# Moving VectorE's two-SBUF-operand additions, and one batch's weight sums, to GpSimd in the softmax stage of a transformer block

## The chip, the cores and the metric

The kernel runs on one core of one Trainium2 chip. A core has a matrix engine (TensorE, "PE" in the profile; its weight loads are listed as "PEld"), three engines for elementwise work (VectorE "DVE", ScalarE "ACT", GpSimd "POOL") and SyncE ("SP"), which here only issues transfers. Each engine runs its own instructions in the order in which the program lists them, and waits on semaphores for the others. The metric is the device time of one execution in microseconds. Three runs of the kernel before took 3894.92, 3904.91 and 3907.19 us.

## The reference

Input x has 8 sequences of 512 tokens by 1024 features, all float32. Four residual steps follow one another, each on a layer norm of what came before:

```python
x = x + attn_a(layernorm(x), qkvw, qkvb, ow, ob)   # 32 heads of 32, softmax over 512 keys
x = x + ffn(layernorm(x), weight, bias, centroids, assignments)
x = x + attn_b(layernorm(x), bv_q, bv_k, bv_v)     # 4 heads of 256, causal, sigmoid in place of softmax
x = x + ffn(layernorm(x), weight, bias, centroids, assignments)

def ffn(h):
    dots = softmax(h @ centroids.T / 0.1)           # 64 clusters
    hits = dots > 0.01
    return where(any(hits, 1)[:, None] & any(hits over all tokens)[assignments], h @ weight.T + bias, 0)
```

The change concerns the first line, the softmax attention: the products for q, k and v (1024 by 3072 weights), scores, softmax, values, the output product with `ow` (1024 by 1024) and its bias, and the first layer norms on both sides of it.

## The kernel before, in words

**Products.** The large products use a scheme of seven products in place of eight for a 2 by 2 split of both factors (`LEFT`, `RIGHT`). Its sums of blocks are `left_sums` and `right_sums`, four additions each; `gather` and `done` add each finished product from PSUM (`acc`) into the outputs that need it. For q, k and v the scheme is nested twice, the inner one over the outer one's nodes. The sums on the side of the weights are made once, while batch 0 runs, and stored to memory: `weight_sums` (L649) for six column groups ("jobs") and two halves `c` each, with lines L669 and L681 as its additions and L672 to L687 its stores.

**The softmax stage** is one generator, `softmax_attention`. It runs 64 units `n`: 8 batches of 8 groups of 4 heads (`NC` = 8 units a batch, g = n % 8), some 41.5 us each. The loop over units (from L1262) does four steps i in each:

- `rows_step(n+1, i)`: TensorE makes 128 rows of scores of the next unit (L1097) in the PSUM tile `sc`, and VectorE takes each row's maximum, `nmax` (L1098);
- `between()`: a share of the auxiliary work, see below;
- at i = 0, `turn_max(n)`: TensorE turns the maxima (`tpm`), of which `split_max` (L1104 to L1108, GpSimd) has made bf16 parts at the end of the unit before; ScalarE casts the result to `shift`;
- `keys_step(n, i)`: TensorE writes the shift (L1126) and the transposed scores (L1129) into `sc`, and ScalarE takes the exponential, `pT` (L1131). `sc` has one PSUM buffer (of four banks), so rows and keys take turns in it;
- `sum_step(n, i)`: GpSimd adds the four `pT` of a unit into `sum` (L1141), two 128x1024 halves at a time. The last sum, and `split_max(n+1)` ahead of it, stand at the end of the unit;
- at i = 0 and 2, `values_step` (L1152) and, at i = 0, `normalize(n-1)`: denominators, reciprocal, and the context `ctx_s` with its bias.

**Auxiliary work** fills the time that a softmax unit leaves on TensorE. `filler` is a queue of pieces with weights (about 0.86 for a matmul group, 0 for work without one); each `take()` runs a fixed share of the queue's total weight (`FILLER_SHARES`). It holds the q, k and v products of coming units and the output products of the batch before. `mix` puts the pieces of a finished row tile's layer norm at given positions of the queue, counted in entries. Two other queues, `side` and `slow`, hold the next batch's layer norm in turned form (`norm_tasks`: load four row tiles, statistics, root, shift, store and spread the per-token factors, load the turned tile, then eight GpSimd operations L628 that scale it). `sums` holds the weight sums, of which each `between` runs one entry.

**The output products.** `out_pair(q)` handles two row tiles, so 14 pairs within the stage and two more at its end. It loads x into `r`, adds the bias `ob_s` (L959), makes the four c sums of the context (L975, two or three `c` tiles and one in place in `ctx_s`), runs seven products and adds them in `done`: `t` (named `ct` in the profile) is a partial result that goes into three quarters of the outputs, r += t (L978). `leave(m)` then stores a finished tile as x1 (L1006) and hands it to the norm (`norm_pieces`, with ScalarE's `rescale` at L264 and the shift at L271). With `OUT_SHARES` = (3, 2, 0, 2) products a unit, leave(0) falls at the end of units with n % 4 = 2 and leave(1) at the end of those with n % 4 = 0, n = 10 to 56, twelve each; the norm of a tile runs in the odd unit behind it.

**The order of GpSimd's instructions** is thus the order in which the generator emits them. At the end of a unit it is: x1 store if there is one, split_max, the two halves of the last sum; the next unit's norm and left sums (L1214) follow.

Both weight streams (`w`, 6 buffers, and `ow`, 5 buffers) are loaded by SyncE's queue, one block for each block that is done.

Of the kernel before, what the change touches and what calls it, by code (L numbers as in the profile page):

```python
# [55 lines left out]
class Consts:  # L56
# [3 lines left out]
    def __init__(self, nc, pool):  # L60
# [3 lines left out]
        nc.vector.memset(self.nhalf, -0.5)  # L64
        self.ones = pool.tile([P, P], F32, name="ones")
# [131 lines left out]
def right_sums(nc, b11, b12, b21, b22, t1, t2, t3, t4):  # L197

    tt = nc.vector.tensor_tensor
    return [  # L200
        partial(tt, t1, b12, b11, ALU.subtract), partial(tt, t2, b22, t1, ALU.subtract),
        partial(tt, t4, b21, t2, ALU.subtract), partial(tt, t3, b22, b12, ALU.subtract),
    ]
# [38 lines left out]
class Stage:  # L242


    def __init__(self, tc, cst, small, ps_m):
        self.tc, self.nc, self.cst, self.small, self.ps_m = tc, tc.nc, cst, small, ps_m

# [6 lines left out]
    def rstd(self, mv, n, r=None):  # L254
# [3 lines left out]
        self.nc.vector.tensor_scalar(r, mv[:, :, 1], EPS, None, ALU.add)  # L258
# [10 lines left out]
    def shifts(self, mv, r, out):  # L269

        self.nc.vector.scalar_tensor_tensor(out, mv[:, :, 0], -1.0, r, ALU.mult, ALU.mult)  # L271
# [57 lines left out]
class Clusters:  # L329
# [41 lines left out]
    def softmax(self, b):  # L371

        nc, small, st = self.stage.nc, self.stage.small, {}
# [5 lines left out]
        def first():  # L379
            top = small.tile([P, TPB], F32, tag="top", name="top")  # L380
            nc.vector.tensor_reduce(top, lg, AX.X, ALU.max)
            nc.vector.tensor_tensor(lg, lg, wide(top), ALU.subtract)
# [4 lines left out]
        def second():  # L387
# [3 lines left out]
            nc.vector.tensor_tensor(lg, lg, wide(den), ALU.mult)  # L391
# [5 lines left out]
        def fourth():  # L397
# [3 lines left out]
            else:  # L401
                some = self.pool.tile([P, NCL], F32, tag="some", name="some")
                nc.vector.tensor_reduce(some, turned, AX.X, ALU.max)
                nc.vector.tensor_max(self.hits, self.hits, some)
# [26 lines left out]
def softmax_attention(tc, cst, stage, filler, clusters, pools, dr, late, args):  # L431
# [28 lines left out]
    units, half = B * NC, NC // 2  # L460
    ctx_s = ctxp.tile([P, SLOTS, half, 2 * P], F32, name="ctx_s")
# [87 lines left out]
    side, slow, tiles, waiting, ready, held = deque(), deque(), deque(), deque(), deque(), []  # L549
# [40 lines left out]
    def norm_tasks(b):  # L590
# [35 lines left out]
        def apply(k, j):  # L626
# [5 lines left out]
            [partial(load, i) for i in range(TPB)],  # L632
            [idle, *(partial(stats, i) for i in range(TPB))],
            [root, partial(turned, 0), shift, partial(turned, 1), send],
            [partial(turned, 2), partial(turned, 3), spread, idle],
# [13 lines left out]
    def weight_sums(kind, job, c):  # L649
# [4 lines left out]
        def load():  # L654
            xs = [npool.tile([P, H], F32, tag=tag, name=f"wx_{kind}_{job}_{c}") for tag in ("n1", "nT")]
# [8 lines left out]
        def outer(k):  # L664
            b21, t4, t2, b12 = (st["x"][i][:, a] for i in range(2) for a in range(2))
            b11, b22 = st["y"][:, 0], st["y"][:, 1]
            if k == 0:
                st["steps"] = right_sums(nc, b11, b12, b21, b22, b11, t2, b12, t4)
            st["steps"][k]()  # L669
            if k == 0:  # L670
                once = dr.once[kind, job].rearrange("p (k c n) -> c p k n", k=2, c=2)
                nc.gpsimd.dma_start(once[c], b11)  # L672

        def again(i, k):
            x = st["x"][i].rearrange("p a k (j n) -> p a k j n", j=2)
            b11, b12, b21, b22 = (x[:, :, kk, j, :] for kk in range(2) for j in range(2))
            if k == 0:
                z = rpool.tile([P, H], F32, tag="r", name=f"wz_{kind}_{job}_{c}_{i}")
                z = st["z"] = z[:, : 3 * 2 * P].rearrange("p (m a n) -> p m a n", m=3, a=2)
                st["more"] = right_sums(nc, b11, b12, b21, b22, z[:, 0], z[:, 1], b12, z[:, 2])  # L680
            st["more"][k]()  # L681
            dst = dr.twice[kind, job, i].rearrange("p (m a c n) -> c a p m n", m=7, a=2, c=2)[c]
            if k == 2:
                for a in range(2):
                    nc.gpsimd.dma_start(dst[a, :, 4:], st["z"][:, :, a, :])
            if k == 3:
                for a in range(2):  # L687
                    nc.gpsimd.dma_start(dst[a, :, :4], x[:, a].rearrange("p k j n -> p (k j) n"))
                if c == 1 and i == 1:
                    stored.add((kind, job))  # L690

        def outers():
            for k in range(4):
                outer(k)

        def agains():
            for i in range(2):
                for k in range(4):
                    again(i, k)

        return [load, lambda: None, outers, agains]
# [89 lines left out]
    def job_pieces(kind, n, part):  # L791
# [24 lines left out]

        def twice(i, k, at):
            def go():
# [13 lines left out]
                weights.done(at)  # L832

# [12 lines left out]
        def done(node, j, acc):  # L846
# [5 lines left out]
            if node == 0:  # L852
                (ia, ja), (ib, jb) = of(0), of(1)
# [3 lines left out]
                add(jb, ib)  # L857
                add(ja, jb, qb)
# [69 lines left out]
    def ow_sum_tasks(c):  # L928
# [8 lines left out]
        def step(k):  # L937
            if k == 0:
                t = [csp.tile([P, half, P], F32, tag=f"c{m}", name="cbox").rearrange("p c t -> p (c t)") for m in range(4)]
                st["t"] = (t[0], t[1], t[3], t[2])  # L940
                st["steps"] = right_sums(nc, st["B11"], st["B12"], st["B21"], st["B22"], *t)
# [5 lines left out]
    def out_pair(q, pools, base, last):  # L947
# [10 lines left out]
        def bias(m):  # L958
            nc.vector.tensor_tensor(r[m], r[m], ob_s, ALU.add)  # L959
# [7 lines left out]
        def sums():  # L967
            a11, a12, a21, a22 = quarters()
            names = (sums_pool.tile([P, half, P], F32, tag=f"c{k}", name=f"c{k}_{q}") for k in range(3))
            st["left"], st["steps"] = left_sums(nc.vector, a11, a12, a21, a22, *names)  # L970
# [6 lines left out]
        def add(out, what):  # L977
            nc.vector.tensor_tensor(out, what, out, ALU.add)  # L978

        def done(k):  # L980
# [7 lines left out]
            elif k == 1:  # L988
                add(st["t"], acc)
                add(r[0][:, b], st["t"])  # L990
# [3 lines left out]
            elif k == 6:  # L994
                add(r[0][:, b], acc)
                leave(0)
            elif k == 3:
                add(st["t"], acc)
                add(r[1][:, a], st["t"])
                add(r[1][:, b], st["t"])  # L1000
            else:
                add(r[1][:, a], acc)
                leave(1)

        def leave(m):
            nc.gpsimd.dma_start(dr.x1[first + m], r[m])  # L1006
# [22 lines left out]
        before = {0: [zero(a11)], 2: [zero(load, 1)], 3: [zero(bias, 1)]}  # L1029
        products = [before.get(idx, []) + [(0.86, mm(idx, c)) for c in range(half)] for idx in range(7)]  # L1030
        for k in range(4):
            products[1].insert(2 * k + 1, zero(some_sum, k))
# [902 lines left out]
```

## Time and profile before

The profiled execution took 3899.21 us, of which 3897.5 us are the span shown in the profile. It is 0.15% below the median of the three runs.

| | us | share of the span |
|---|---|---|
| TensorE busy | 3675.3 | 94% |
| VectorE busy | 2569.3 | 66% |
| GpSimd busy | 1634.9 | 42% |
| ScalarE busy | 940.5 | 24% |
| granted TensorE clock, mean | 0.984 | |

Softmax stage: about 0 to 2720 us. The remaining 1178 us are the later steps of the block.

| stretch, us | TensorE busy | granted clock |
|---|---|---|
| 0 to 320 | 286.99 | 0.98 |
| 320 to 500 | 152.47 | 0.92 |
| 500 to 2460 | 1840.78 | 0.99 |
| 2460 to 2720 | 232.76 | 0.97 |
| 2720 to 3897 | 1162.29 | 1.00 |

In lines of the profile, `sc<-qk,qk` is an output and its inputs by the program's names, the numbers that follow are partitions by elements. In a line of the waits, the three numbers are the total in us, how many, and the longest. In a line of a group, `| 31.8, 2119 |` is busy time in us and the mean of one in ns, then the idle time ahead of them and what ended it. In a line of the timeline, the first two numbers are the start and the length in us, and the brackets hold the idle time just before and what released it.

### The profile page before, as it was taken

The page shows a single profiled execution, that of the slowest core. Times are in us where ns is not written, and L with a number is a line of the kernel's source. Part 1 is how long each engine was busy: PE and PEld are TensorE (multiplying, and loading weights), DVE is VectorE, ACT ScalarE, POOL GpSimd, SP SyncE. Part 2 cuts the span into 40 slices and gives each one's busy share as a digit, 9 for nine tenths or more (in the row PEclk, how much of TensorE's full clock was granted, in tenths as well). Part 3 has the DMA queues.
Part 4 walks back from the last instruction along what each step waited for, and adds up shares of the span by engine and source line. Part 5 has one row for each costly group of instructions (what it writes and reads, how often), then busy time and mean ns, then how long its engine had stood idle before and what let it go on. Part 6 is the DMA issues. An engine that isn't in the chain of part 4 may idle for free.

```text
span 3897.5 us, 81316 instructions
## 1 busy us (share of the span) xinstructions
PE 3675.3 (94%) x34228; PEld 1929.0 (49%) x34228; DVE 2569.3 (66%) x3649; ACT 940.5 (24%) x1047; POOL 1634.9 (42%) x1378
## 2 busy tenths in 40 slices
PE   8998899999999999999999999998999999999999
PEld 4345454545545454454544445533444457774444
DVE  4657666677667757667675766665698864556666
ACT  1222222222222222222222222323111134431000
POOL 2875565466455545635554563443000034540000
PEclk9999999999999999999999999999999999999999
DMA  5657756666665665766566565536566667774332
GB/s 178 179 173 236 230 163 188 190 180 176 180 188 145 206 182 168 207 160 177 160 204 178 156 182 158 145 114 195 188 175 178 175 185 226 224 232 146 130 129 97
DMA packets 756954, 690.11 MB, mean 177 GB/s; under 512 B 327912, under 2 KB 563440, under 8 KB 756592
## 3 DMA queue, kind: packets, MB, share of 16 engines
q1 hardware_dynamic: 725328, 575.07, 52.4%
q0 software_dynamic: 26944, 94.13, 6.6%
q10 hardware_dynamic: 4320, 15.73, 1.0%
q8 instruction: 271, 4.44, 0.5%
q14 instruction: 91, 0.75, 0.1%
HBM read 537.94 MB, written 146.83 MB: 176 GB/s over the span
## 4 chain that ended last, share of the span: by engine, by line
PE 79%; DVE 12%; DMA 4%; issue 2%; POOL 2%; ACT 1%; SPq 0%; DVEq 0%; ACTq 0%; POOLq 0%
PE mm L647 31%; PE dense L1496 20%; PE av L1152 6%; PE sc L1129 5%; PE sc L1097 5%; DVE nmax L1098 4%; PE o L1577 3%; PE csc L1558 3%; PE sc L1126 2%; DMA w<-in_qkvw 2%; DVE r L978 1%; PE logitsT L349 1%; PE den L1191 1%; DVE qk L842 1%; DVE r L959 1%
## 5 line engine op out<-in xcount | busy, mean ns | idle before, releaser
L1131 ACT ACTIVATE pT<-sc 128x2048 f32<-128x2048 f32 x256 | 480.6, 1878 | 1246.8 <-PE sc L1129 1235.6
L1141 POOL TENSOR_TENSOR sum<-sum,pT 128x1024 f32<-128x1024 f32 x256 | 613.2, 2417 | 332.9 <-ACT pT L1131 332.8
L1098 DVE TENSOR_REDUCE nmax<-sc 128x4 f32<-128x2048 f32 x256 | 585.1, 2285 | 156.3 <-PE sc L1097 156.2
L1141 POOL TENSOR_TENSOR sum<-pT,pT 128x1024 f32<-128x1024 f32 x128 | 325.7, 2568 | 546.6 <-ACT pT L1131 305.8
L647 PE MATMUL mm<-xT,w 128*64 128x128 f32 (+6 forms) x4164 | 390.8, 344 | 22.6 <-DMA w<-in_qkvw 20.1
L647 PEld LDWEIGHTS mm<-xT,w 128*64 128x64 f32 (+2 forms) x4164 | 229.2, 132 | 188.2 <-issue 112.2
L647 PE MATMUL mm<-s,w 128*64 128x256 f32 (+3 forms) x3288 | 288.1, 351 | 25.8 <-issue 13.1
L1097 PE MATMUL sc<-qk,qk 32*64 32x512 f32 x4096 | 289.3, 621 | 1.7 <-ACT pT L1131 1.5
L1129 PE MATMUL sc<-qk,qk 32*128 32x512 f32 x2048 | 270.5, 601 | 0.0
L163 DVE TENSOR_TENSOR u<-dense,u 128x512 f32<-128x512 f32 x223 | 148.0, 685 | 185.0 <-PE dense L1496 169.5
L647 PE MATMUL mm<-ow,ctx_s 128*64 128x512 f32 (+2 forms) x1168 | 262.3, 600 | 4.4 <-DMA ow<-o_T 3.9
L647 PEld LDWEIGHTS mm<-s,w 128*64 128x64 f32 (+1 forms) x3288 | 175.5, 129 | 179.9 <-issue 68.0
L1152 PE MATMUL av<-pT,v 128*32 128x512 f32 x2048 | 255.8, 619 | 0.0
L1496 PE MATMUL dense<-sum,s 128*128 128x512 f32 x512 | 231.8, 593 | 0.0
L647 PEld LDWEIGHTS mm<-e,w 128*64 128x64 f32 (+1 forms) x3456 | 178.6, 134 | 84.8 <-issue 41.6
L647 PE MATMUL mm<-e,w 128*64 128x128 f32 (+1 forms) x3456 | 206.5, 278 | 11.8 <-DVE qk L163 6.5
L163 DVE TENSOR_TENSOR qk<-mm,qk 128x256 f32<-128x256 f32 x392 | 157.9, 417 | 80.2 <-PE mm L647 72.9
L647 PE MATMUL mm<-w,xT 128*64 128x128 f32 (+4 forms) x2816 | 194.0, 296 | 3.7 <-DMA w<-t_v 3.7
L1126 PE MATMUL sc<-shift,ones_h 32*128 32x512 bf16 x1024 | 102.8, 390 | 98.7 <-DVE nmax L1098 91.8
L163 DVE TENSOR_TENSOR v<-mm,v 128x256 f32<-128x256 f32 x196 | 78.6, 417 | 164.5 <-PE mm L647 159.3
L647 PEld LDWEIGHTS mm<-w,xT 128*64 128x64 f32 (+2 forms) x2816 | 150.8, 133 | 63.3 <-issue 29.3
L647 PE MATMUL mm<-ow,c 128*64 128x512 f32 (+2 forms) x816 | 178.2, 597 | 2.1 <-DMA ow<-o_T 2.1
(267 smaller groups left out, 5501.6 us busy)
## 6 DMA issues: line engine op xcount, KB each, us to landing
w<-t_qk SPq DMA_DIRECT2D x392, 256.0 KB, 3.5
ow<-o_T SPq DMA_DIRECT2D x240, 256.0 KB, 4.0
w<-in_qkvw SPq DMA_DIRECT2D x216, 256.0 KB, 4.5
w<-t_v SPq DMA_DIRECT2D x196, 256.0 KB, 2.8
ow<-in_ow SPq DMA_DIRECT2D x180, 256.0 KB, 3.2
dT_a<-xT SPq DMA_DIRECT2D x32, 512.0 KB, 6.2
x_a<-x SPq DMA_DIRECT2D x32, 512.0 KB, 7.9
x<-x_a POOLq DMA_DIRECT2D x32, 512.0 KB, 4.5
```

What stands on the lines that cost most here:

```text
L163: nc.vector.tensor_tensor(out, acc, other, ALU.add)
L647: nc.tensor.matmul(out[cols], lhsT[:, cols], rhs, **flags)
L1097: nc.tensor.matmul(sc[ts(j, P // 2), h, :], st["q"][rows, cols], st["k"][rows, :], start=True, stop=True)
L1098: nc.vector.tensor_reduce(st["nmax"][:, qt, :], sc, AX.X, ALU.max, negate=True)
L1126: nc.tensor.matmul(sc[:, h, :], cst.ones_h[rows, :], st["shift"][rows, :], start=True, stop=False)
L1129: nc.tensor.matmul(sc[:, h, :], st["k"][rows, ts(kt, P)], st["q"][rows, :], start=False, stop=True)
L1131: nc.scalar.activation(pT, sc, AF.Exp, scale=SCALE_A)
L1141: nc.gpsimd.tensor_tensor(st["sum"][:, h, :], before[:, h, :], st["pT", kt][:, h, :], ALU.add)
L1152: nc.tensor.matmul(st["av"][rows, :], st["v"][:, kt, rows], pT[:, h, :], start=(kt == 0), stop=(kt == TPB - 1))
L1496: nc.tensor.matmul(st["acc"], st["left"][LEFT[k]][:, c, :], self.w[RIGHT[k]][:, c, :], start=(c == 0), stop=(c == half - 1),)
L1558: nc.tensor.matmul(sc[:, AT_OFF[i] : AT_OFF[i] + n], k[:, c, ts(i, P)], xT[:, c, i * P :], start=(c == 0), stop=(c == 1),)
L1577: nc.tensor.matmul(acc[:, j - jj, :], at[:, start : start + P], self.v[b * TPB + i][:, cols], start=(i == 0), stop=(i == j),)
```

## The change

Within the softmax stage, these parts move or are rewritten:

- `stage.few` is GpSimd while the stage runs and VectorE after it: the addition of eps, the layer norm's shift (now two multiplications, with constants `eps` and `minus`), and the subtraction, scaling and collecting of the cluster softmax.
- `weight_sums`: its additions go to GpSimd, its nine stores a half from GpSimd's queue to SyncE's; they are paced in three entries a (job, c) instead of four, and c = 1 uses other buffers.
- Batch 0 (n < 8): the additions of kt = 2 and 3 in `sum_step` become one 128x2048 addition on VectorE; that of kt = 3 stands in the next unit, ahead of its first rows_step.
- Nested node 0: VectorE adds from PSUM alone; four additions of 128x256 a pair or group (`join`) are left for GpSimd, emitted at the next `between` or before the outer node 0 is added.
- `out_pair`, for the 14 pairs of the stage: the four c sums go to GpSimd and from product 1, where they were spaced out, to the start of product 0. The additions of `t` into the three quarters (`join`) and the bias go to GpSimd and stand in `done` and `leave`, just before the store of x1.
- The sums of `ow` go to GpSimd.
- The loads, statistics and turned loads of the next batch's norm are spread differently over four entries.
- The turned tile of a finished row tile is fetched at filler position 26 instead of 20.

In instructions: VectorE goes from 3168 to 2735, GpSimd from 1013 to 1488, SyncE from 1883 to 1990; TensorE and ScalarE keep theirs, with a few in another order.

```diff
 # class Stage, rstd and shifts
-        self.nc.vector.tensor_scalar(r, mv[:, :, 1], EPS, None, ALU.add)
+        self.few.tensor_tensor(r, mv[:, :, 1], self.cst.eps[:, :n], ALU.add)
         self.nc.gpsimd.tensor_tensor(r, r, self.cst.nhalf[:, :n], ALU.pow)
...
-        self.nc.vector.scalar_tensor_tensor(out, mv[:, :, 0], -1.0, r, ALU.mult, ALU.mult)
+            self.few.tensor_tensor(out, mv[:, :, 0], self.cst.minus[:, : mv.shape[1]], ALU.mult)
+            self.few.tensor_tensor(out, out, r, ALU.mult)
 # softmax of clusters
-            nc.vector.tensor_tensor(lg, lg, wide(top), ALU.subtract)
+            few.tensor_tensor(lg, lg, wide(top), ALU.subtract)
 # norm_tasks
-            [partial(load, i) for i in range(TPB)],
-            [idle, *(partial(stats, i) for i in range(TPB))],
-            [root, partial(turned, 0), shift, partial(turned, 1), send],
-            [partial(turned, 2), partial(turned, 3), spread, idle],
+            [partial(load, 0), idle, partial(load, 1), idle, partial(load, 2)],
+            [partial(stats, 0), partial(load, 3), partial(stats, 1), partial(stats, 2), idle],
+            [partial(stats, 3), partial(turned, 0), root, partial(turned, 1), shift],
+            [send, partial(turned, 2), spread, partial(turned, 3), idle],
 # weight_sums
-                st["steps"] = right_sums(nc, b11, b12, b21, b22, b11, t2, b12, t4)
+            for step in right_sums(nc.gpsimd, b11, b12, b21, b22, b11, t2, b12, t4):
+                step()
...
-                nc.gpsimd.dma_start(once[c], b11)
+            nc.sync.dma_start(dr.once[kind, job].rearrange("p (k c n) -> c p k n", k=2, c=2)[c], st["y"][:, 0])
 # job_pieces
+        def join(j, side):
+            nc.gpsimd.tensor_tensor(target(side, j)[:, 1], target(1, j)[:, side == 0], target(side, j)[:, 1], ALU.add)
...
+                if all(len(m) == 7 for m in made):
+                    soon.extend(partial(join, j, side) for j in range(2) for side in (1, 0))
...
-                add(jb, ib)
-                add(ja, jb, qb)
+                add(jb, acc)
+                add(ja, acc, qb)
 # out_pair
         def bias(m):
-            nc.vector.tensor_tensor(r[m], r[m], ob_s, ALU.add)
+            engine.tensor_tensor(r[m], r[m], ob_s, ALU.add)
...
-            st["left"], st["steps"] = left_sums(nc.vector, a11, a12, a21, a22, *names)
+            st["left"], st["steps"] = left_sums(engine, a11, a12, a21, a22, *names)
...
+        def join(out):
+            engine.tensor_tensor(out, st["t"], out, ALU.add)
...
             elif k == 1:
                 add(st["t"], acc)
-                add(r[0][:, b], st["t"])
...
             elif k == 6:
                 add(r[0][:, b], acc)
+                join(r[0][:, b])
                 leave(0)
             elif k == 3:
                 add(st["t"], acc)
-                add(r[1][:, a], st["t"])
-                add(r[1][:, b], st["t"])
             else:
                 add(r[1][:, a], acc)
+                join(r[1][:, a])
+                join(r[1][:, b])
                 leave(1)
 
         def leave(m):
+            bias(m)
             nc.gpsimd.dma_start(dr.x1[first + m], r[m])
...
         for k in range(4):
-            products[1].insert(2 * k + 1, zero(some_sum, k))
+            products[0].insert(1 + k, zero(some_sum, k))
 # sum_step
+        if kt > 1 and n < NC:
+            nc.vector.tensor_tensor(st["sum"], st["sum"], st["pT", kt], ALU.add)
+            return
 # the unit loop
-        for _ in range(2 if n < half - 1 or n == start else 1):
+        for _ in range(2 if n < half - 1 or n == NC - 1 else 1):
...
+            if i == 0 and 0 < n <= NC:
+                sum_step(n - 1, TPB - 1)
...
-        sum_step(n, TPB - 1)
+        if n >= NC:
+            sum_step(n, TPB - 1)
```

## The prediction

> **What bounds the kernel now.** I read the first part of the page (busy time by engine), then the waits in front of TensorE, then the groups of instructions by form, then the timeline at those waits.
>
> ```profile
> PE 3675.3 (94%) x34228; PEld 1929.0 (49%) x34228; DVE 2569.3 (66%) x3649; ACT 940.5 (24%) x1047; POOL 1634.9 (42%) x1378
> 500.00:2460.00 1960.00, 1840.78 (x23052) 975.66 (x23050) 1333.62 (x1829) 506.45 (x512) 1013.00 (x712) 0.99 0.62 177
> PE sc L1126 <- DVE nmax L1098: 91.8, 67, 5.2
> PE mm L647 <- DMA w<-in_qkvw: 26.3, 13, 5.1
> PE tpm L647 <- POOL parts L1108: 12.9, 26, 3.0
> ```
>
> TensorE is busy 94% of the span. The second line is the steady softmax stage, 500 to 2460 us (length, then busy PE, PEld, DVE, ACT, POOL, granted clock, DMA share, GB/s): TensorE idles 119 of 1960 us. The same view gives 287.0 busy of the first 320 us, 152.5 of the next 180 and 232.8 of the 260 after 2460: 33 + 27.5 + 119 + 27 = 207 us of idle TensorE in the stage. That caps what an unchanged TensorE program can win, the clock aside. The waits (us, times, longest) show what could be had: 91.8 us where the exponent scores wait for a row maximum, 26.3 us for weight loads. The last wait, for `parts`, is small: 0.5 us each, but it is the one to watch.
>
> ```profile
> L975 DVE TENSOR_TENSOR c<-c,ctx_s 128x512 f32<-128x512 f32 x15 | 31.8, 2119 | 0.1
> L959 DVE TENSOR_TENSOR r<-r,ob_s 128x1024 f32<-128x1024 f32 x30 | 60.5, 2017 | 0.0
> L978 DVE TENSOR_TENSOR r<-mm,r 128x512 f32<-128x512 f32 x90 | 60.6, 687 | 106.6 <-PE mm L647 99.8 <-ACT ct L984 6.9
> L628 POOL TENSOR_TENSOR xT<-xT,rows 128x1024 f32<-128x1024 f32 x56 | 133.7, 2398 | 4.6 <-DMA w<-in_qkvw 3.3
> L1214 POOL TENSOR_TENSOR e<-xT 128x512 f32<-128x512 f32 x14 | 19.0, 1357 | 0.0
> L1214 POOL TENSOR_TENSOR e<-xT 128x256 f32<-128x256 f32 x7 | 5.1, 732 | 0.0
> 1140.89 2.58 DVE L975 TENSOR_TENSOR c<-c,ctx_s 128x512 f32<-128x512 f32 x1
> 1143.39 2.28 DVE L1098 TENSOR_REDUCE nmax<-sc 128x4 f32<-128x2048 f32 x1
> 1145.72 0.40 PE L1126 MATMUL sc<-shift,ones_h 32*128 32x512 bf16 x4 [2.70 <-DVE nmax L1098]
> ```
>
> The group lines give mean ns after the bar. A 128x512 add takes VectorE 687 ns with one operand in PSUM, 2119 with two in SBUF while GpSimd works. The timeline's last three lines are such a case: a c sum of 2.58 us holds up the row maximum and TensorE waits 2.70 us. So the change attacks a real loss.
>
> **Gains, part by part.** (1) c sums to GpSimd: 11 places in 500 to 2460 with waits of 2.7 us, -30. (2) The other waits for the maximum there (58.9 in all, by node-0 adds, the joins into r and the bias): -29. (3) Spread norm loads: the in_qkvw waits, -26 (between 0 and 26.3). (4) Waits for VectorE's qk adds (9.5 at L163, 7.6 at L842): -8, about half, as their PSUM operand stays. (5) Batch 0 (to 500 us: 18.2 for the maximum, 15.6 for other VectorE operations, 10.7 for loads): -25, as GpSimd gets 33 to 47 us of work in units of some 40. Its 128x2048 adds on VectorE are in no row: twice a 128x1024, 2 x 1.22 alone to 2 x 2.02 contended; I take 2.4, ahead of a unit's first row maximum, inside that 25. (6) After 2460: 14.7, take -10. Together -128, between 0 and -207. The softmax-of-clusters, eps and shift operations are tiny on either engine (229 to 235 ns on GpSimd) and the moved DMA issues cost 0.55 to 0.6 us each, off GpSimd and onto SyncE: nothing by themselves; what counts is what they queue behind. Node 0's extra joins on GpSimd (4 x 0.73 a pair) are new work beside TensorE's products; I find no reader that waits for them except in the five units named below.
>
> **Losses: GpSimd's queue at a unit's end.** In the built instruction order, the last join, the bias and the x1 store of a row tile now stand on GpSimd before `split_max` of the next unit. In before, GpSimd had been waiting there for the same last VectorE add:
>
> ```profile
> 1284.16 0.61 POOL L1006 DMA_DIRECT2D x<-r  x1 [8.44 <-DVE r L978]
> 1284.77 0.34 POOL L1104 CAST parts<-nmax 128x16 bf16<-128x16 f32 x1
> 1286.11 0.25 POOL L1108 CAST parts<-rest 128x16 bf16<-128x16 f32 x1
> 1286.26 4.70 POOL L1141 TENSOR_TENSOR sum<-sum,pT 128x1024 f32<-128x1024 f32 x2
> 1290.91 0.56 POOL L259 TENSOR_TENSOR ln_rstd<-ln_rstd,nhalf 128x1 f32<-128x1 f32 x1
> 1286.42 0.41 PE L647 MATMUL tpm<-ident_h,parts 128*64 128x128 bf16 x8 [0.35 <-POOL parts L1108]
> 1294.16 1.11 PE L1097 MATMUL sc<-qk,qk 32*64 32x512 f32 x16
> 1289.93 1.88 ACT L1131 ACTIVATE pT<-sc 128x2048 f32<-128x2048 f32 x1 [2.47 <-PE sc L1129]
> 1296.20 1.24 ACT L264 ACTIVATE n<-r,ln_shift,ln_rstd 128x1024 f32<-128x1024 f32 x1 [0.40 <-DVE ln_shift L271]
> ```
>
> TensorE's `tpm` starts 0.06 us after the split's last cast and already waited 0.35: no slack. I found this in exactly the 24 odd units (11 to 57) that follow a store; the others have about 6 us. VectorE's add ends near 1284.1, and the first join and the bias need its result. So each microsecond put ahead of the split is one on TensorE: leave(0) one join 128x512 (1.28, the shortest GpSimd row; the mean is 1.36) and a bias of 128x1024 (2.37) = 3.65; leave(1) two joins = 4.95. 12 x 3.65 + 12 x 4.95 = **+103** (bounds: 0 if the two joins and bias ran in the 8.44 us gap, excluded by the wait; 24 x 5.5 = 132 if each runs slower beside VectorE).
>
> **Losses: the rescale ahead of the first exponential.** The four c sums now are entries of weight zero at the start of product 0, so the filler positions 2, 7 and 14 come earlier in the unit. In the built order the rescale (L264) of 11 units (13, 17, ... 53) moves from behind `exp(0)` (L1131 at 1289.93; the rescale at 1296.20) to before it, and it waits for GpSimd's shift. ScalarE runs in order, `exp(0)` waits behind it, the one PSUM buffer `sc` is not free, and TensorE stands at rows_step(1). Unit 29 above, counted from 1284.1: two joins 2.6, bias 2.4, store 0.6, split 1.6, the last sum 4.7, eps and pow 0.8 (1296.8); then two left sums of 2.37, four of 0.73, two c sums of 1.33 and the shift 0.5 (1307.6); rescale 1.24, exp 1.88: 1310.7. rows_step(1) was at 1294.16 and would be at 1299.1 with the tpm late by 4.95: a stall of 11.6. In units 17, 25, 33, 41, 49 two applies (4.74) stand there instead of the 7.66 of sums: 8.7. 6 x 11.6 + 5 x 8.7 + 4 (unit 57, which has fewer sums) = **+117**. Bounds: 0 if the shift were made within the 2.47 us that ScalarE waits there anyway, against GpSimd's queue as counted; 150 if GpSimd's operations run a tenth slower. In units 19, 27, 35, 43, 51 the cluster softmax's exponential waits in the same way for a subtraction that is now on GpSimd behind the split, the sum and four v joins (4 x 0.73): 2.9 each, **+15** (0 to 25).
>
> **The clock.** A TensorE idle is followed by a slower stretch:
>
> ```profile
> 1222.30:1226.50 4.20, 4.20 (x44) 2.42 (x46) 2.95 (x4) 0.00 (x0) 1.43 (x1) 0.61 0.23 62
> ```
>
> This 4.2 us, granted 0.61, follows an idle of 2.61 us; after one of 2.71 at 1310 the clock stayed at 1.00. The mean clock of 0.984 means at most 62 us lost in the span. Such stretches at half clock last 3.4 us in the trace, 1.7 us of lost work. There would be 41 new idles of 2.9 us and more (24 + 12 + 5) against 16 removed: (41 - 16) x 1.7 = 42 at most, 0 at least, taken 30, as not every idle is followed by one. The Trainium skill, "TensorE: Matmul & The Clock Gate", section "What's actually happening", says that the array halves its clock only after an idle window of about 3.4 us. The trace halves it after 2.6, so the measurement decides here; by the page the removed waits gave nothing back and the 36 long ones cost 61, and the sum would be 4067.
>
> The same skill's "GPSIMD Engine Reference", section 4.1 with 3.1, speaks against the change: elementwise work belongs on VectorE, as GpSimd is 1.96 times slower. The rows here say 1357 against 687 alone (1.98, agreed) but the four c sums together cost VectorE 2119 + 1846 + 1327 + 678 = 5970 ns beside GpSimd and 4 x 1357 = 5428 on it. By the page gain (1) would be a loss on GpSimd; by the row it is a gain, and what decides is the queue.
>
> **Sum.** 3899.2 (the profiled execution: span 3897.5 and 1.7 around it; 0.15% below the median 3904.9 of the runs) - 128 + 103 + 117 + 15 + 30 = **4036**.
>
> **Rivals.** (a) Faster: GpSimd's work lies in its idle time and neither split nor rescale reaches TensorE, because the last VectorE add comes earlier once VectorE has lost its 2 us operations. For it: GpSimd is idle 947 of the 1960 us, 20 of each unit's 41.5. Against: the add follows TensorE's last product (99.8 us of its idle are waits for `mm`), so it can't come earlier. It decides if the add ends 5 us sooner. Time: 3899 - 128 = 3771, less up to 25 of clock: 3750 to 3790. Chance 0.11. (b) Only the late split counts, the rescale is hidden: 3899 - 128 + 103 + 15 = 3889, 3870 to 3925. Chance 0.06. For it: that rescale wait lies on ScalarE, 24% busy. (c) It spreads: batch 0 carries GpSimd's backlog of 5 to 8 us over several units, SyncE's stores of the weight sums wait for it at the head of the queue of TensorE's weight loads (12 jobs x 5 = 60), and every new idle costs clock (42): above 4140. Chance 0.13. (d) The norm loads don't end the in_qkvw waits: +26, within my range.
>
> **How the numbers follow.** My forecast (3930 to 4140) has 0.70, (c) 0.13, (a) 0.11, (b) 0.06. The range 3930 to 4165 leaves out (a), (b) and the far end of (c), 0.2. Under 0.3% (12 us) two versions can't be told apart here. Faster: (a) and half of (b); same 0.03; slower 0.83.
>
> **What would show it.** Right: waits of `tpm` for POOL `parts` of 4 to 5.5 us, 24 of them; in 11 units a TensorE idle of 9 to 12 us before the second row scores, with the rescale right before it on ScalarE, itself waiting for POOL; waits of L1126 for `nmax` under 40 us; VectorE's share under 60%, GpSimd's over 48%. Wrong: `tpm` waits unchanged near 0.5 us, or the rescale ending before the scores of keys_step(0) are there.

## The result, and the profile after

The changed kernel takes 4010.41 us (median of 4 runs, 4006.43 to 4013.99) against 3900.55 us for the kernel before in the same comparison: a ratio of 1.0281, with a 95% interval of 1.0258 to 1.0303. It is 110 us slower. Its profiled execution has a span of 4004.6 us, 107.1 longer than the one of before.

The first part of its page, busy time by engine:

```profile
PE 3698.2 (92%) x34232; PEld 1950.8 (49%) x34232; DVE 2215.2 (55%) x3291; ACT 936.1 (23%) x1047; POOL 1930.2 (48%) x1817
```

VectorE lost 354 us of work and GpSimd took 295. (The profile lists 3649 instructions on VectorE before and 3291 after, 1378 and 1817 on GpSimd; the counts given with the change are not these.) TensorE, which sets the time, has 22.9 us more busy time for the same products, and idles 306.4 instead of 222.2: 84.2 + 22.9 = 107.1. Where the idle time lies is in the waits in front of TensorE (total us, times, longest):

```profile
PE tpm L657 <- POOL parts L1127: 129.1, 27, 8.5
PE sc L1116 <- ACT pT L1150: 90.7, 20, 9.6
PE sc L1145 <- DVE nmax L1117: 16.2, 21, 2.1
PE tp L310 <- ACT n L269: 11.2, 4, 5.4
PE den L1213 <- POOL sum L1163: 8.7, 2, 8.3
PE mm L657 <- DMA w<-t_qk: 8.5, 2, 6.1
PE mm L657 <- DVE qk L167: 5.9, 3, 3.5
```

Of the kernel before, the waits for the maximum, the loads and `parts` stand ahead of the prediction's gains; the row scores had this line:

```profile
PE sc L1097 <- ACT pT L1131: 1.5, 6, 0.5
```

Read beside these, the lines show that what the change aimed at has gone: the wait for row maxima fell from 91.8 to 16.2 us, and the wait for in_qkvw loads, 26.3 before, no longer has a line. Two new waits outweigh it. `tpm` went from 12.9 to 129.1, and the row scores, which now wait for ScalarE's exponential, from 1.5 to 90.7.

The groups of instructions by form show what the moved operations cost (busy us, then mean ns, then the idle time ahead of them and its cause):

```profile
L990 POOL TENSOR_TENSOR c<-c,ctx_s 128x512 f32<-128x512 f32 x14 | 17.7, 1264 | 0.9
L996 POOL TENSOR_TENSOR r<-ct,r 128x512 f32<-128x512 f32 x42 | 52.7, 1268 | 171.2 <-DVE r L993 171.2
L974 POOL TENSOR_TENSOR r<-r,ob_s 128x1024 f32<-128x1024 f32 x28 | 65.6, 2344 | 2.2
```

A c sum that took VectorE 2119 ns beside GpSimd takes GpSimd 1264. The length of the operations is not the problem; their place is. GpSimd idles 171.2 us before the joins, until VectorE's last addition, and that is not new. In the kernel before it waited for the same addition ahead of the store of x1:

```profile
POOL x L1006 <- DVE r L978: 225.6, 28, 25.1
```

New is what stands behind that wait: the joins and the bias, ahead of the split and of everything else in the queue. The timeline of unit 29 of the changed kernel shows it on GpSimd, and then on TensorE and ScalarE (start, length, then in brackets the idle time before and its end):

```profile
1308.76 2.50 POOL L996 TENSOR_TENSOR r<-ct,r 128x512 f32<-128x512 f32 x2 [6.97 <-DVE r L993]
1311.34 2.34 POOL L974 TENSOR_TENSOR r<-r,ob_s 128x1024 f32<-128x1024 f32 x1
1313.97 0.63 POOL L1025 DMA_DIRECT2D x<-r  x1 [0.30 <-POOL r L974]
1314.60 0.26 POOL L1123 CAST parts<-nmax 128x16 bf16<-128x16 f32 x1
1315.86 0.25 POOL L1127 CAST parts<-rest 128x16 bf16<-128x16 f32 x1
1316.01 4.66 POOL L1163 TENSOR_TENSOR sum<-sum,pT 128x1024 f32<-128x1024 f32 x2
1331.75 0.19 POOL L280 TENSOR_TENSOR ln_shift<-ln_shift,ln_rstd 128x1 f32<-128x1 f32 x1
...
1316.16 0.64 PE L657 MATMUL tpm<-ident_h,parts 128*64 128x128 bf16 x8 [5.28 <-POOL parts L1127]
1335.04 2.01 PE L1116 MATMUL sc<-qk,qk 32*64 32x512 f32 x16 [8.46 <-ACT pT L1150]
...
1331.98 1.24 ACT L269 ACTIVATE n<-r,ln_shift,ln_rstd 128x1024 f32<-128x1024 f32 x1 [14.55 <-POOL ln_shift L280]
1333.12 1.86 ACT L1150 ACTIVATE pT<-sc 128x2048 f32<-128x2048 f32 x1
```

The split starts 5.8 us after the first join, and TensorE has waited 5.28 us for them. Then the rescale waits 14.55 us for the shift, the exponential behind it comes only at 1333.12, and TensorE stands 8.46 us for the `sc` buffer. In the same unit before, these two waits were 0.35 and 0.

### The profile page after: what moved, and what is told of

It reads as the page before. It is cut to its first block, busy times and chain, and to the rows that moved or that the text cites. A ratio compares the mean times of both kernels' runs of the same rounds, so it can differ in the third digit from the quotient of the medians.

```text
span 4004.6 us, 81530 instructions
## 1 busy us (share of the span) xinstructions
PE 3698.2 (92%) x34232; PEld 1950.8 (49%) x34232; DVE 2215.2 (55%) x3291; ACT 936.1 (23%) x1047; POOL 1930.2 (48%) x1817
## 4 chain that ended last, share of the span: by engine, by line
PE 78%; POOL 12%; DVE 3%; DMA 2%; issue 2%; ACT 1%; SPq 1%; POOLq 0%; ACTq 0%; DVEq 0%
PE mm L657 32%; PE dense L1529 19%; PE sc L1116 6%; PE sc L1148 5%; PE av L1174 5%; PE o L1610 3%; PE csc L1591 3%; POOL sum L1163 2%; PE sc L1145 2%; POOL r L974 2%; PE logitsT L358 1%; POOL r L996 1%; DVE nmax L1117 1%; ACT pT L1150 1%; PE den L1213 1%
## 5 line engine op out<-in xcount | busy, mean ns | idle before, releaser
L1163 POOL TENSOR_TENSOR sum<-sum,pT 128x1024 f32<-128x1024 f32 x224 | 523.9, 2360 | 246.3 <-ACT pT L1150 246.2
L1163 POOL TENSOR_TENSOR sum<-pT,pT 128x1024 f32<-128x1024 f32 x128 | 299.4, 2360 | 466.9 <-ACT pT L1150 374.2
L657 PE MATMUL mm<-xT,w 128*32 128x128 f32 (+6 forms) x4356 | 387.5, 339 | 0.4 <-issue 0.4
L1116 PE MATMUL sc<-qk,qk 32*64 32x512 f32 x4096 | 295.1, 633 | 90.9 <-ACT pT L1150 90.7
L657 PE MATMUL mm<-s,w 128*64 128x256 f32 (+3 forms) x3288 | 284.2, 347 | 12.9 <-DMA w<-t_qk 6.1
L657 PEld LDWEIGHTS mm<-s,w 128*64 128x64 f32 (+1 forms) x3288 | 175.0, 128 | 160.4 <-issue 59.4
L657 PEld LDWEIGHTS mm<-e,w 128*64 128x64 f32 (+1 forms) x3248 | 212.2, 157 | 81.5 <-issue 61.3
L657 PE MATMUL mm<-e,w 128*64 128x128 f32 (+1 forms) x3248 | 240.9, 310 | 3.9 <-DMA w<-t_qk 2.5
L1216 DVE STREAM_TRANSPOSE rden<-den 128x512 f32<-128x512 f32 x64 | 45.9, 717 | 261.3 <-PE den L1213 255.8
L657 PEld LDWEIGHTS mm<-w,xT 128*64 128x64 f32 (+2 forms) x2824 | 150.1, 132 | 59.4 <-issue 25.4
```

Source lines behind the costliest of these rows:

```text
L657: nc.tensor.matmul(out[cols], lhsT[:, cols], rhs, **flags)
L1116: nc.tensor.matmul(sc[ts(j, P // 2), h, :], st["q"][rows, cols], st["k"][rows, :], start=True, stop=True)
L1163: nc.gpsimd.tensor_tensor(st["sum"][:, h, :], before[:, h, :], st["pT", kt][:, h, :], ALU.add)
```

## The experiments

All times below are medians, with the ratio to the kernel before from the same comparison and its 95% interval. The kernel before had medians of 3891.75 to 3900.55 us in them, so a difference to the changed kernel is given both by the ratios (of 3900) and by the medians. The theory is the prediction's: the loss comes from the places that the moved operations took in GpSimd's queue. The rival is that it comes from GpSimd's load or from its collisions with VectorE, so that the order matters little.

### The split ahead of the joins

```diff
+            if i == TPB - 1 and n + 1 < units:
+                split_max(n + 1)
             between(False, HD_A if i in (0, 2) and n > 0 else 2 * HD_A)
-        if n + 1 < units:
-            split_max(n + 1)
```

> The changed kernel with split_max of the next unit emitted just ahead of the last between of a unit, so that GpSimd makes the bf16 parts before the last join, the bias and the store. Queue theory: the 24 waits of tpm (12 x 4.05 and 12 x 5.28, 112 us) disappear, but the total falls by less: GpSimd's instructions ahead of the norm's shift are as many as before, so the 11 rescales end at the same time while TensorE arrives 5 us sooner: the idles at rows_step(1) grow from 8.6 and 6.9 to about 13.5 and 12 (+57), those behind the cluster softmax from 0.9 to about 4.9 (+20). 4010 - 112 + 57 + 20 - 10 of clock = about 3965 us. Rival (GpSimd's total load or its collisions with VectorE slow the stage, not the place in the queue): time and idles as in the changed kernel, 4000 to 4020 us.

Measured: 3963.49 us, ratio 1.0184 (1.0158 to 1.0209). The waits in front of TensorE:

```profile
PE sc L1116 <- ACT pT L1150: 119.1, 21, 11.5
PE den L1213 <- POOL sum L1163: 53.2, 38, 8.3
PE tpm L657 <- POOL parts L1127: 16.9, 3, 8.1
```

The 24 waits of `tpm` are gone (the three left are in batch 0), 112 us of them, but the kernel gained only 38 to 47. The rest came back behind the next thing in the queue, as expected in sum and not quite as expected in its parts: the row scores' wait grew by 28 us instead of 77, and a wait of 44 us that was not foreseen appeared, of the denominators for the last sum, which still stands behind join, bias and store. A wait taken off an engine's queue is handed to what stands behind it. With the same operations on the same engines, the rival foresaw no gain at all.

### The shift back on VectorE

```diff
-        self.few.tensor_tensor(r, mv[:, :, 1], self.cst.eps[:, :n], ALU.add)
+        self.nc.vector.tensor_scalar(r, mv[:, :, 1], EPS, None, ALU.add)
...
-        if self.few is self.nc.vector:
-            self.few.scalar_tensor_tensor(out, mv[:, :, 0], -1.0, r, ALU.mult, ALU.mult)
+        if True:
+            self.nc.vector.scalar_tensor_tensor(out, mv[:, :, 0], -1.0, r, ALU.mult, ALU.mult)
```

> The changed kernel with the layer norms' eps and shift back on VectorE, so that the rescale no longer stands behind the left sums and c sums on GpSimd, only behind the square root there. Queue theory: the 11 idles at rows_step(1) of 8.6 and 6.9 us (91 us in all) shrink to about 1 us each, the tpm waits stay at 4.05 and 5.28: 4010 - 80 - 6 of clock = about 3924 us. Rival (load and collisions): tiny operations moved, so 4000 to 4015 us with the idles unchanged.

Measured: 3906.15 us, ratio 1.0039 (1.0025 to 1.0054). The waits in front of TensorE:

```profile
PE tpm L657 <- POOL parts L1127: 129.8, 28, 8.1
PE sc L1116 <- ACT pT L1150: 12.8, 16, 1.4
```

And its busy time by engine, from the page:

```profile
PE 3675.1 (94%) x34232; PEld 1940.0 (50%) x34232; DVE 2242.2 (57%) x3364; ACT 936.6 (24%) x1047; POOL 1910.5 (49%) x1709
```

Moving back operations of 0.2 us each is worth 94 to 104 us. 78 of them are the wait for the exponential (90.7 to 12.8). The page's line holds most of the rest: TensorE's busy time is down from 3698.2 to 3675.1, 23 us, for the same matmuls. The trace's records of the granted clock fit that: added up over the time in which TensorE is busy, the work lost to a clock below 1.00 falls from 91.2 to 69.3 us. So the clock's part was larger than the 6 us expected here.

### The c sums back at product 1, still on GpSimd

```diff
-            products[0].insert(1 + k, zero(some_sum, k))
+            products[1].insert(2 * k + 1, zero(some_sum, k))
```

> The changed kernel with the four c sums, still on GpSimd, back at product 1 and spaced. The rescale then stands behind the first exponential on ScalarE, as in the kernel before, though its shift is still made by GpSimd. Queue theory: the idles at rows_step(1) (91 us) go to under 10 us in all, tpm waits stay at 4.05 and 5.28: 4010 - 85 - 8 of clock = about 3917 us. Rival (load and collisions; the same GpSimd instructions): 4000 to 4015 us.

Measured: 3898.72 us, ratio 1.0007 (0.9994 to 1.0021). The waits in front of TensorE:

```profile
PE tpm L657 <- POOL parts L1127: 129.0, 27, 7.6
PE sc L1116 <- ACT pT L1150: 10.5, 12, 3.2
```

Every operation is on the engine where the change put it; the c sums are moved to a later point in the unit, by which the rescale comes behind the first exponential again (in unit 29 ScalarE starts the exponential at 1286.54 us and the rescale at 1293.78). 107 to 112 us are gained by that one line, and the kernel is level with the one before. This shows that the place, not the engine, made the second loss.

### A second bias ahead of the split

```diff
         def leave(m):
             bias(m)
+            if engine is nc.gpsimd:
+                bias(m)
```

> The changed kernel with the bias of the stage's 14 pairs added twice, so its output has the output bias once too often in those tiles: 2.37 us more of GpSimd ahead of each split. Queue theory: each of the 24 tpm waits grows by 2.37 (to 6.4 and 7.65), rows_step(1) and the rescale move alike, so those idles stay: 4010 + 57 + up to 8 of clock = 4067 to 4075 us. Rival (GpSimd has 20 us free in a unit, the queue's order does not matter): 4010 to 4020 us.

Measured: 4080.39 us, ratio 1.0486 (1.0464 to 1.0508). The waits in front of TensorE:

```profile
PE tpm L657 <- POOL parts L1129: 188.5, 27, 8.6
PE sc L1118 <- ACT pT L1152: 92.6, 19, 9.5
```

The `tpm` wait grew by 59.4 us, 58 of them in the 24 units, for 24 operations of 2.34 us (56), the row scores' by 2, and the time by 70 to 80. What is put ahead of the split is paid by TensorE one to one, though GpSimd is idle half of the span.

### One part alone: joins and bias on GpSimd

The kernel before, with nothing of the change but this:

```diff
         def bias(m):
-            nc.vector.tensor_tensor(r[m], r[m], ob_s, ALU.add)
+            engine.tensor_tensor(r[m], r[m], ob_s, ALU.add)
...
-                add(r[0][:, b], st["t"])
...
+                join(r[0][:, b])
                 leave(0)
...
-                add(r[1][:, a], st["t"])
-                add(r[1][:, b], st["t"])
...
+                join(r[1][:, a])
+                join(r[1][:, b])
                 leave(1)
...
         def leave(m):
+            bias(m)
             nc.gpsimd.dma_start(dr.x1[first + m], r[m])
...
```

> The kernel before with one part of the change alone: the 14 pairs' additions of t into r and their biases go to GpSimd, just before the store of x1, ahead of split_max. Queue theory: the 24 waits of tpm go from 0.4 to about 4 and 5.3 us (+105), the maxima behind the joins and biases come sooner (-15), the clock takes some 10; the rescale stays behind the first exponential, so no idles at rows_step(1): 3894 + 100 = about 3995 us (3975 to 4015). Rival (what counts is that VectorE loses its two-operand additions): 3894 - 15 = about 3880 us and tpm waits as before.

Measured: 3993.24 us, ratio 1.0251 (1.0223 to 1.0278). The waits in front of TensorE:

```profile
PE tpm L647 <- POOL parts L1112: 117.2, 26, 6.1
PE sc L1130 <- DVE nmax L1102: 79.2, 45, 7.1
PE mm L647 <- DMA w<-in_qkvw: 19.2, 11, 3.9
```

The wait for maxima fell by 12.6 us and `tpm` rose by 104: this part alone loses 2.5% where the whole change loses 2.8%; the rest of the change, its gains and the second loss together, comes to little.

### One part alone: the norm loads spread

The kernel before, with the four lines of `norm_tasks` and the loop's `n == NC - 1` from the change.

> The kernel before with one part of the change alone: the next batch's norm loads, statistics and turned loads spread as in the changed kernel. If the norm's bunched loads delay the weight loads: the 26.3 us of waits for in_qkvw end and the time is about 3868 us. Rival (those waits only move to other weight loads, or are made up later): 3885 to 3900 us.

Measured: 3879.75 us, ratio 0.9964 (0.9940 to 0.9988). The waits in front of TensorE:

```profile
PE sc L1126 <- DVE nmax L1098: 96.3, 68, 7.5
PE mm L647 <- issue: 17.6, 8, 3.5
PE mm L647 <- DMA w<-in_qkvw: 4.6, 3, 2.0
```

Between the two: the loads' wait fell by 21.7 us, 4.5 each came back as waits for maxima and in TensorE's own queue, and some 14 to 19 us remain (0.36% by the ratio).

### Three edits: the split first, the shift on VectorE, the rescale later

The first two experiments' edits together, and

```diff
-        filler.mix(norm[:2], 0 if near else 2, 2 if near else 5)
+        filler.mix(norm[:2], 0 if near else 2, 2 if near else 9)
```

> The changed kernel with three edits: split_max ahead of a unit's last between, the norm's eps and shift on VectorE, and the rescale four filler positions later (behind the first exponential). Queue theory: tpm waits (112 us) and idles at rows_step(1) (91 us, and the growth that the early split alone brought) go; what the early split alone also brought stays, the denominators' wait for the last sum, which still stands behind join, bias and store (44 us, 38 times), and the cluster softmax's subtraction may hold the first exponential in five units (up to +20): 3906 (shift on VectorE alone) - 112 + 44 - 10 of clock = about 3828 us, 3815 to 3850. Rival (the two losses hide one another's, and a third wait of GpSimd's load takes over): about 3900 us.

Measured: 3844.66 us, ratio 0.9860 (0.9839 to 0.9881): within the range, 17 us above the forecast. The wait of the denominators for the last sum stayed, 53.9 us in 38 places, and was the longest one left.

### The last sum first as well

```diff
-    stage.few = nc.gpsimd
...
+            if i == TPB - 1:
+                if n + 1 < units:
+                    split_max(n + 1)
+                if n >= NC:
+                    sum_step(n, TPB - 1)
             between(False, HD_A if i in (0, 2) and n > 0 else 2 * HD_A)
-        if n + 1 < units:
-            split_max(n + 1)
-        if n >= NC:
-            sum_step(n, TPB - 1)
```

and the rescale at its later position.

> As the three edits together, and besides a unit's last sum stands, behind split_max, ahead of the last between too, and all the small operations (eps, shift, cluster softmax) are on VectorE again. GpSimd's 8 us of waiting for the last addition into r then take in the split and the last sum. Queue theory: neither tpm nor the denominators wait any more, the rescale's root comes 3 us sooner: 3906 - 112 - 8 - 12 of clock = about 3775 us, 3760 to 3800. Rival (GpSimd's load is the bound): no gain over the three edits.

Measured: 3786.51 us, ratio 0.9717 (0.9696 to 0.9737). Run once more, 3785.17 us, ratio 0.9726 (0.9711 to 0.9740):

> The same kernel as e10_sum_first, beside e11_batch0_back on the same chip: 3783 to 3793 us, as before.

The timeline of GpSimd at one unit's end:

```profile
1234.98 0.25 POOL L1126 CAST parts<-rest 128x16 bf16<-128x16 f32 x1
1237.32 4.68 POOL L1162 TENSOR_TENSOR sum<-sum,pT 128x1024 f32<-128x1024 f32 x2 [2.09 <-ACT pT L1149]
1241.95 2.50 POOL L995 TENSOR_TENSOR r<-ct,r 128x512 f32<-128x512 f32 x2
1244.53 2.37 POOL L973 TENSOR_TENSOR r<-r,ob_s 128x1024 f32<-128x1024 f32 x1
1248.75 0.56 POOL L264 TENSOR_TENSOR ln_rstd<-ln_rstd,nhalf 128x1 f32<-128x1 f32 x1 [0.94 <-DVE ln_rstd L263]
```

The joins' group, the `tpm` waits and the busy times by engine:

```profile
L995 POOL TENSOR_TENSOR r<-ct,r 128x512 f32<-128x512 f32 x42 | 52.9, 1274 | 5.0 <-DVE r L992 5.0
PE tpm L656 <- POOL parts L1126: 15.9, 3, 8.0
PE 3652.9 (96%) x34232; PEld 1915.7 (51%) x34232; DVE 2258.1 (60%) x3381; ACT 937.9 (25%) x1047; POOL 1906.5 (50%) x1692
```

The split and the last sum now stand in the time in which GpSimd waited for VectorE, and the joins have waited once, 5.0 us, where they waited 171.2. The two large losses are gone (the three `tpm` waits left are in batch 0, and the row scores wait 0.8 us in all): this version is 2.7 to 2.8% faster than the kernel before and some 5.5% faster than the changed one (0.9717 of 1.0281), with GpSimd nearly as busy as there (1906.5 us of 1930.2). The rival, by which GpSimd's load or its collisions make the loss, falls by that.

### Batch 0's part undone

The last version, with the additions of the weight sums on VectorE and batch 0's sums of exponentials on GpSimd again:

```diff
-            for step in right_sums(nc.gpsimd, b11, b12, b21, b22, b11, t2, b12, t4):
+            for step in right_sums(nc.vector, b11, b12, b21, b22, b11, t2, b12, t4):
...
-            for step in right_sums(nc.gpsimd, b11, b12, b21, b22, z[:, 0], z[:, 1], b12, z[:, 2]):
+            for step in right_sums(nc.vector, b11, b12, b21, b22, z[:, 0], z[:, 1], b12, z[:, 2]):
...
-        if kt > 1 and n < NC:
-            nc.vector.tensor_tensor(st["sum"], st["sum"], st["pT", kt], ALU.add)
-            return
...
```

> As e10 (split and last sum first, small operations on VectorE, rescale later), but batch 0's part of the change undone on the engines: the weight sums' additions on VectorE again and batch 0's sums of the exponentials on GpSimd again; the stores stay on SyncE. In the changed kernel batch 0 gained only 7 us by unit 8 (its tpm came at 413.5 instead of 420.8), with 16 us of new tpm waits in units 1 to 3 against 13.7 us of fewer waits for maxima. If that is a trade of one wait for another, this kernel comes within 8 us of e10 (3780 to 3795), with tpm waits of batch 0 near 4 us and waits for maxima near 17. If the move in batch 0 is worth the 25 us that were forecast, it comes to about 3810.

Measured: 3789.82 us, ratio 0.9736 (0.9722 to 0.9749), 4.7 us above the last version in the same comparison, with overlapping intervals. Batch 0's waits in front of TensorE, to 415 us, of this version and then of the last one:

```profile
PE sc L1144 <- DVE nmax L1116: 36.9, 10, 10.2
PE mm L656 <- DVE qk L167: 6.6, 1, 6.6
```

```profile
PE tpm L656 <- POOL parts L1126: 17.6, 3, 8.8
PE mm L656 <- DMA w<-t_qk: 10.7, 2, 7.5
PE mm L656 <- DVE qk L167: 7.0, 3, 3.2
PE sc L1144 <- DVE nmax L1116: 3.1, 3, 1.8
```

Here the change trades 33.8 us of waits for maxima (36.9 to 3.1) against 28.3 of waits for GpSimd and for stored weight sums (17.6 and 10.7); the waits for VectorE's qk additions stay. (In the version that is undone, the waits for maxima are not quite those of before, 16.8, as the pacing differs.)

## Why the prediction was right

The direction, the mechanism and the place were as predicted; the time was 26 us below the forecast of 4036. By its terms, from the profiled executions:

- **The late split, +103.** Right, within 2 us. The waits of `tpm` in the twelve units after leave(0) are 4.04 to 4.07, and after leave(1) 5.27 or 5.28 in ten of twelve (5.75 and 6.12 in the others), of which 0.24 to 0.59 had been there before, and 1.22 in unit 57. Without batch 0 the line rose from 8.7 to 113.2 us, by 105. That this is a matter of order is shown by moving the split (the 24 waits gone) and by the second bias (58 for 56).
- **The rescale, +117.** The right 11 units, and too much: 85 us, 8.4 to 9.6 in the units for which 11.6 was worked out, 5.5 to 7.0 where 8.7 was; of the 9 to 12 us that the prediction named as a sign, one unit of the 11 shows it (9.62). The chain on GpSimd and ScalarE was right: the exponential of unit 29 ended 18.8 us after `tpm` began, 19.3 was worked out. What was wrong is TensorE's own arrival: it was taken to need 7.7 us from `tpm` to the second row scores, as before, and needed 10.4. The windows (length, busy PE, PEld, DVE, ACT, POOL, granted clock, DMA share, GB/s) say why: first unit 29 of the kernel before from its `tpm` on, then of the changed kernel the same stretch and the one behind the row scores' wait.

```profile
1286.40:1291.00 4.60, 4.58 (x52) 2.07 (x56) 3.03 (x7) 1.66 (x2) 4.60 (x3) 1.00 0.97 373
1316.20:1321.70 5.50, 5.50 (x52) 4.28 (x52) 0.85 (x2) 0.58 (x1) 5.42 (x5) 0.50 0.31 75
1335.10:1340.00 4.90, 4.90 (x44) 2.71 (x46) 2.85 (x3) 0.49 (x1) 2.09 (x3) 0.63 0.02 5
```

  Behind the `tpm` wait the clock was 0.50 for the next 5.5 us, and what TensorE lost by that, some 2.7 us, it did not have to wait a second time. The prediction had moved TensorE's arrival by the 4.95 us of the `tpm` wait itself; what it left out is the slow stretch behind it, which it counted in the clock's term alone. The 4 us for unit 57 did not come.
- **The cluster softmax, +15.** The mechanism showed, at a third of the size: 0.9 us instead of 2.9 in each of those units that has it in the timeline, four of five, for the same reason (TensorE came 9.4 us after `tpm` in those four instead of 7.7).
- **The gains, -128.** Idle time rose by 84 us; the lines that grew (tpm 116, row scores 89, the final transposes' and denominators' waits some 16) make 221, so all others shrank by 137. Of these 75.6 are the maxima, 26.3 the in_qkvw loads, 11 the waits for VectorE's qk additions. But batch 0, for which 25 were put in (its waits for loads are 10.9 us by the lines, not 10.7), gave 7: `tpm` of unit 8 came at 413.5 us instead of 420.8, and new waits for GpSimd of 4.3, 8.5 and 3.1 us in units 1 to 3 took the rest. The last experiment agrees. In the end of the stage and after it (from unit 57's tpm on) the changed kernel loses 8 us where 10 of gain were put in. In between, from unit 8 to unit 57, it grew by 106 us: 105 + 85 + 4 of the new waits and 28 more of TensorE's busy time (1902.4 to 1930.2) make 222, so the gains there were some 116 where 93 were put in. Together the gains were some 115 of the 128; that the total is so near is in part luck, as the stretch between made up for most of what batch 0 and the end did not give.
- **The norm loads.** In the changed kernel the wait for them is gone; alone, this part was worth 14 to 19 us and not 26.
- **The clock, +30.** 22.9 us by TensorE's busy time; added up from the clock's records over that time, the loss rose from 55.6 to 91.2 us, by 36. What made the busy time shorter elsewhere by the difference is not known. In the changed kernel the 4 us behind an idle of over 3 us had a granted clock of 0.50 to 0.65 in 26 of 27 cases of `tpm` and in all 11 of the row scores. Before, 14 of 21 idles of 2.5 to 2.9 us were followed by 0.57 to 0.66 and seven by 1.00. The stretches below 1.00 were also longer than the 3.4 us that the prediction took: before, 24 of 31 last 3.4 us, in the changed kernel 24 of 47 last 6.8. The rule quoted from the Trainium skill, "TensorE: Matmul & The Clock Gate", section "What's actually happening", that only an idle window of some 3.4 us halves the clock, would have made the term 61; it fits the long idles and not those 14. The experiments give a rough price for the two groups: with the shift on VectorE, which takes the row scores' idles away, TensorE's busy time is 3675.1 us, and with the last sum first, where the others are gone too, 3652.9, so about 23 and 22 us (by the clock's records 22 and 29). Busy time is not the clock alone: with the three edits, which end both groups as well, it is 3681.3 us at a loss of 47.9 to the clock.

Of the rivals, the faster one needed the last addition into `r` to come 5 us sooner; it did not: in unit 29 GpSimd still idles 6.97 us before it, against 8.44 before, and counted from `tpm` of unit 28 the addition came 1.5 us sooner. The second, in which only the split counts, is what the c sums at product 1 make of the kernel: 3898.72, where 3889 was given. The third, in which GpSimd's lateness spreads, had its start in batch 0 (16 us) and went no further. The fourth, that the norm loads' waits stay, did not come about.

## What to carry to other kernels

An engine that is idle half of the time still has a queue, and an operation moved to it is priced by what stands behind it, not by its length: look at who reads the next results of that queue and how much slack that reader has. Where an engine waits in order for a late operand, put the work that is due next ahead of that wait; here the same operations, with the split and the last sum emitted earlier, the rescale later and the small ones left on VectorE, turn a loss of 2.8% into a gain of 2.7 to 2.8%. Two stalls that follow one another on one engine should not simply be added: the first, and the slow clock behind it, let the engine arrive later at the second and take from it.

## What was not expected of the hardware

An idle of 4 to 5 us costs TensorE about a third as much again where no later wait takes it up: in the experiment with the joins and bias alone, 104 us of new waits in 24 idles came with a busy time of 3711.2 instead of 3675.3 us, 36 us more, or 1.5 us each. By the clock's records the loss while TensorE is busy rose there from 55.6 to 99.2 us. Some 10 us had been expected of the clock in that experiment.
